# Moving the loads of the gates' weights and of y into the first batch, and the first filter stores to SyncE

## The chip, the cores and the metric

One core of a Trainium2 chip. The time is the device time of one call in microseconds (us), median of several runs. The kernel before took 1970.6 us (1967.1 to 1972.8), so one run alone says little about less than 3 us.

Names in the profile: PE is TensorE's matmul, PEld its weight load, DVE VectorE, ACT ScalarE, POOL GpSimd, SP SyncE. A q behind an engine's name is its sequencer, which issues transfers. A half-rate window is a stretch for which the trace gives PE's granted clock as 0.5; before the kernel's end such windows last 3.4 us each, and some come two in a row (6.8 us). Work at half rate takes twice its time, so 3.4 us of it cost 1.7 us. L404 is a line of the kernel; since all matmuls are recorded by one helper, matmuls are told apart by their tiles (`acc<-V,wb`).

## The reference, cut to what matters

A layer norm and a ReLU over x of shape (64, 256, 256), then one graph layer per graph: a 1-wide and a 17-wide convolution with batch norms, a message pass over `A = exp(-dist) * adj`, and a GRU.

```python
h = jnp.maximum(_layernorm(x, axis=-1), 0.0)
...
    h = _bn(_conv1d(h, conv2_w, 8), bn2_g, bn2_b, bn2_m, bn2_v)      # 17 taps
    x_conv = jnp.transpose(jax.nn.relu(h + xc), (0, 2, 1))
    ...
    gi = x_in @ w_ih.T + b_ih
    gh = x @ w_hh.T + b_hh
    ...
    return (1.0 - z) * nn_ + z * x
# x = x + that
```

## The kernel before

The 17-wide convolution is done by a short transform along the sequence (VectorE), products per frequency (TensorE) and the transform back. The 57 steps of `filters` compute the transformed filters on TensorE, ScalarE copies each result to one of six `fo` buffers, and a store puts it into device memory. `load_bin` later reads the filter of one frequency back as a tile `wb` (768 KB), of which there are three buffers. The filters are computed once; the batches (8 batches of 4 pairs of graphs) follow.

```python
    def filters(m, g):
        ...
        t = stage.tile([P, W], FP, name="fo", bufs=6)
        nc.scalar.copy(t[:size * kinds], p[:size * kinds])
        (nc.gpsimd if g % 2 else nc.sync).dma_start(
            out=filt[m][g * KG:g * KG + size].rearrange("k t c o -> (k t) (c o)"), in_=t[:size * kinds])
...
    for j in range(PB):                      # the first batch's convolutions; 4 filter steps in each
        ...
        for m, n in steps[j * 4:(j + 1) * 4]:
            filters(m, n)
    forward()                                # queues VectorE's odd and even transforms
    for j, (m, n) in enumerate(steps[PB * 4:]):      # the other 41 filter steps
        filters(m, n)
        if j + PB * 4 == 2 * NG - 10:
            load_bin(0, 0)
            load_bin(0, 1)
    nc.scalar.dma_start(out=w_hh, in_=hh_wT.rearrange("(k p) o -> p k o", p=P))
    nc.scalar.dma_start(out=w_ih, in_=ih_wT.rearrange("(k p) o -> p k o", p=P))
    ...
    load_y(0)                                # x once more, for the residual: GpSimd's queue
    load_y(1)
    pace.flush(odd)                          # VectorE: the odd transform
    s2, h2_shift = fold_bn(bn2, "bn2", 1.0 / L)      # VectorE, one pow on GpSimd, VectorE
    ...
    for b in range(NB):
        i = b * PB
        embed(i)
        products(b, 0)                       # the even transform is put between these on VectorE
        message(i)
        products(b, 1)
        affinity(i)                          # ends with GpSimd's load of the next adj
        embed(i + 1)
        products(b, 2)
        transpose_a(i)
        products(b, 3)
        aggregate(i)
        products(b, 4)
        message(i + 1)
        products(b, 5)
        affinity(i + 1)
        ...                                  # products 6 and 7, then gates(): first use of w_hh, w_ih
```

Of the kernel before, what the change touches and what calls it, by code (L numbers as in the profile page):

```python
# [297 lines left out]
def kernel(  # L298
# [26 lines left out]
    nc = tc.nc  # L325
    P = 128
# [43 lines left out]
    def load_rows(t, src, i, eng):  # L370
        for g in range(G):
            eng.dma_start(out=row_tile(t, g), in_=rows(src, G * i + g))  # L372
# [9 lines left out]
    def load_y(i):  # L382
        Y[i] = late.tile([P, G * MC, D], FP, name="y", bufs=2)
        load_rows(Y[i], x, i, nc.gpsimd)
# [18 lines left out]
    def mm(p, w, v, columns, **kw):  # L403
        nc.tensor.matmul(p, w, v, **kw)  # L404
        pace.tensor(columns)
# [87 lines left out]
    for n, bins in enumerate(PASSES):  # L493
        f = filter_points(bins, TAPS)
        m = np.zeros((KG, TAPS, KG, f.shape[1]), np.float32)
# [26 lines left out]
    def aux():  # L522
        return psum.tile([P, W], FP, name="aux", bufs=3)

    def acc():
        return psum.tile([P, W], FP, name="acc", bufs=5)
# [41 lines left out]

    filt = [dram.tile([P, t.shape[1] // KG, DC, D], FP, name=f"filt{n}") for n, t in enumerate(points)]

    def filters(m, g):

        kinds = filt[m].shape[1]
        size = min(KG, P - g * KG)
        p = acc()
        for dc in range(DC):
            mm(p[:size * kinds, dc * D:(dc + 1) * D], points[m][:size * TAPS, :size * kinds],
               taps[:size * TAPS, g, dc, :], D, start=True, stop=True)
        t = stage.tile([P, W], FP, name="fo", bufs=6)
        nc.scalar.copy(t[:size * kinds], p[:size * kinds])  # L580
        (nc.gpsimd if g % 2 else nc.sync).dma_start(  # L581
            out=filt[m][g * KG:g * KG + size].rearrange("k t c o -> (k t) (c o)"), in_=t[:size * kinds])


# [2 lines left out]
    def load_bin(b, n):  # L587
        b, n = b + n // BINS, n % BINS
        if b < NB:
            WB[b, n] = work.tile([P, 3, DC, D], FP, name="wb", bufs=3)  # L590
            kinds, m = 3 if n < BINS - 1 else 2, n // len(PASSES[0])
            first = 3 * (n - PASSES[m][0])
            nc.sync.dma_start(out=WB[b, n][:, :kinds], in_=filt[m][:, first:first + kinds])
# [15 lines left out]
    def products(b, m):  # L609
        load_bin(b, 2 * m + 2)  # L610
        p = [acc() for _ in range(3)]
        for n in range(2):
            for kind, v in enumerate(operands(2 * m + n)):
                if v is None:
                    continue
                for o in range(DC):
                    for k in range(DC):
                        mm(p[kind][:, (n * DC + o) * P:(n * DC + o + 1) * P],
                           WB[b, 2 * m + n][:, kind, k, o * P:(o + 1) * P],
                           v[:, k::DC, 0, :], P, start=(k == 0), stop=(k == DC - 1))  # L620
        load_bin(b, 2 * m + 3)
        p1 = work.tile([P, W], FP, name="p1")
        pv = [t.rearrange("p (n a e) -> p a n e", n=2, e=NW) for t in (p1, p[1], p[2])]
        if m < 7:
            nc.scalar.copy(p1, p[0])
            if m < 4:
                re, im = Yv(m % 2, m // 2 * 2, 2), Yv(m % 2, 4 + m // 2 * 2, 2)
            elif m < 6:
                re, im = Yu(m - 4, 0, 2), Yu(m - 4, 2, 2)
            else:  # L630
                t = Yu.t[:, :, :, 6:8, :].rearrange("p a c n e -> p n a c e")
                re, im = t[:, 0], t[:, 1]
            pace.vector(2 * W, pace.pe + PSUM)
            nc.vector.tensor_sub(re, pv[0], pv[2])
            nc.vector.tensor_add(im, pv[0], pv[1])
        else:
            half = W // 2
            nc.scalar.copy(p1[:, :half], p[0][:, :half])
            nc.scalar.mul(Yu(0, 4)[:, :, 0, :], p[0][:, half:].rearrange("p (a e) -> p a e", e=NW), 0.5)
            nc.scalar.mul(Yu(1, 4)[:, :, 0, :], p[1][:, half:].rearrange("p (a e) -> p a e", e=NW), 0.5)  # L640
            pace.vector(W, pace.pe + PSUM)
            nc.vector.tensor_sub(Yu(0, 5)[:, :, 0], pv[0][:, :, 0], pv[2][:, :, 0])
            nc.vector.tensor_add(Yu(1, 5)[:, :, 0], pv[0][:, :, 0], pv[1][:, :, 0])
# [59 lines left out]
    def aggregate(i):  # L703
        XNM[i] = late.tile([P, DC, W], FP, name="xnm", bufs=2)
        for dc in range(DC):
            p = aux()
            for g in range(G):
                for c in range(MC):
                    mm(graph(p, g), MSG[i][:, g, c, dc * P:(dc + 1) * P], AT[i][:, g, c, :], N,
                       start=(c == 0), stop=(c == MC - 1))  # L710
            nc.scalar.activation(XNM[i][:, dc, :], p, AF.Copy)
# [76 lines left out]
    w_ih = const.tile([P, 2 * DC, 3 * D], FP)  # L788
    w_hh = const.tile([P, DC, 3 * D], FP)
# [17 lines left out]
    for j in range(PB):  # L807
        if j > 0:
            transpose_h(j)
        if 0 < j < PB - 1:  # L810
            norm(j + 1)
        conv1(j)
        run(split_steps(j))
        for m, n in steps[j * 4:(j + 1) * 4]:
            filters(m, n)
    forward()
    for j, (m, n) in enumerate(steps[PB * 4:]):
        filters(m, n)
        if j + PB * 4 == 2 * NG - 10:
            load_bin(0, 0)  # L820
            load_bin(0, 1)
    nc.scalar.dma_start(out=w_hh, in_=hh_wT.rearrange("(k p) o -> p k o", p=P))
    nc.scalar.dma_start(out=w_ih, in_=ih_wT.rearrange("(k p) o -> p k o", p=P))
    stage_ctx.close()
    late = ctx.enter_context(tc.tile_pool(name="late", bufs=1, reuse_waits="tile"))
    Yvt = late.tile([P, SL], FP, name="Yv")
    Yv = Slots(Yvt, GB * DC, L // 2, NW)
    load_y(0)
    load_y(1)
    pace.flush(odd)  # L830
    s2, h2_shift = fold_bn(bn2, "bn2", 1.0 / L)
    b_rz = const.tile([P, 2 * DC], FP)
# [5 lines left out]
    for b in range(NB):  # L838
        i = b * PB
        nxt = i + PB  # L840
        embed(i)
        pace.flush(odd)
        products(b, 0)
        message(i)
        products(b, 1)
        pace.add(fft.branch_back(Yv, T, 0))
        affinity(i)
# [3 lines that stand above are left out]
        if b > 0:  # L851
            finish(i - 1)
        products(b, 3)
        pace.flush(even)
        pace.add(fft.branch_back(Yv, T, 2))
        pace.add(fft.odd_back(Yv, T))
        aggregate(i)
        products(b, 4)
        message(i + 1)
        products(b, 5)  # L860
        pace.add(mix(fft.q_back(Yu, T), fft.odd_factors(Yv)))
        affinity(i + 1)
        norm(nxt)
        products(b, 6)
        transpose_a(i + 1)
        products(b, 7)
        pace.add(mix(fft.p_back(Yu, T), fft.q_factors(Yu)))

        def join(j):
            pace.add(fft.join(Yu, Yv, T, slice(2 * G * j, 2 * G * (j + 1))))  # L870
            pace.add([(W, lambda o=o: residual(i + j, o)) for o in range(DC)], joined[j])
        stats, scale = norm_steps(nxt + 1)
        join(0)
        pace.add(stats)
        join(1)
        pace.add(scale, normed)
        pace.add(split_steps(nxt), halved)
        join(2)
        join(3)
        aggregate(i + 1)  # L880
        transpose_h(nxt)
        embed(i + 2)
        message(i + 2)
        conv1(nxt)
        affinity(i + 2)

        def wait(j=0):
            pace.flush(joined[j])
        gates(i, 0, wait)
        transpose_a(i + 2)  # L890
        gates(i, 1)
        pace.flush(normed)
        transpose_h(nxt + 1)
        aggregate(i + 2)
        pace.flush(halved)
        conv1(nxt + 1)
        stats, scale = norm_steps(nxt + 2)
        pace.add(stats)
        pace.add(split_steps(nxt + 1), halved)
        pace.add(scale, normed)  # L900
        pace.flush(joined[1])
        gates(i + 1, 0)
        pace.flush(normed)
        transpose_h(nxt + 2)
        message(i + 3)
        embed(i + 3)
        conv1(nxt + 2)
        stats, scale = norm_steps(nxt + 3)
        pace.add(stats)
        pace.add(split_steps(nxt + 2), halved)  # L910
        pace.add(scale, normed)
        finish(i)
        gates(i + 1, 1)
        affinity(i + 3)
        gates(i + 2, 0)
        pace.flush(normed)
        transpose_h(nxt + 3)
        transpose_a(i + 3)
        conv1(nxt + 3)
        pace.add(split_steps(nxt + 3), halved)  # L920
        if b + 1 < NB:
            forward()
        finish(i + 1)
        gates(i + 2, 1)
        aggregate(i + 3)
        gates(i + 3, 0)
        finish(i + 2)
        gates(i + 3, 1)
# [46 lines left out]
```

## Time and profile before

| | before |
|---|---|
| time, median | 1970.6 us |
| span of the profiled run | 1969.0 us |
| PE busy | 1918.9 us (97 %) |
| PE's waits after the first filter store, to 220 us | 10.6 us in nine places, 0.6 of them for hT in two |
| PE's waits after 220 us | 2.2 us |

PE is the bound nearly everywhere, so the span splits at two landmarks. The last filter matmul starts at 112.16 us. From there to the first gates' matmul (`acc<-hT,w_hh`, at 197.83 us) it is 85.7 us. From there to the end it is 1771.2 us. The change touches only the first two stretches. The profile's lines stand in the prediction, with their reading. Two names in it: msg is the operation of VectorE that empties one of three `aux` buffers, for which PE waits; the fold (`fold_bn`) is the string of tiny operations that makes scale and shift of the second batch norm, with bn_scale on GpSimd in its middle.

### The profile page before, as it was taken

The page shows a single profiled execution, that of the slowest core. Times are in us where ns is not written, and L with a number is a line of the kernel's source. Part 1 is how long each engine was busy: PE and PEld are TensorE (multiplying, and loading weights), DVE is VectorE, ACT ScalarE, POOL GpSimd, SP SyncE. Part 2 cuts the span into 40 slices and gives each one's busy share as a digit, 9 for nine tenths or more (in the row PEclk, how much of TensorE's full clock was granted, in tenths as well). Part 3 has the DMA queues.
Part 4 walks back from the last instruction along what each step waited for, and adds up shares of the span by engine and source line. Part 5 has one row for each costly group of instructions (what it writes and reads, how often), then busy time and mean ns, then how long its engine had stood idle before and what let it go on. Part 6 is the DMA issues. An engine that isn't in the chain of part 4 may idle for free.

```text
span 1969.0 us, 21300 instructions
## 1 busy us (share of the span) xinstructions
PE 1918.9 (97%) x7972; PEld 1209.2 (61%) x7972; DVE 1402.3 (71%) x2668; ACT 641.9 (33%) x1050; POOL 184.9 (9%) x277
## 2 busy tenths in 40 slices
PE   4899999999999999999999999999999999999997
PEld 2678555875459655695557855496546955478543
DVE  2769738996489946998379964899559984699522
ACT  1443322343222432235222433124322253234321
POOL 3210000010100000010000101001010100000000
PEclk9999999999999999999999999999999999999999
DMA  5776011540216212270115402163122711144010
GB/s 177 224 233 185 22 43 59 182 129 22 70 35 224 74 43 59 86 223 24 43 48 165 156 12 70 42 207 93 32 70 59 241 36 34 32 132 143 4 43 22
DMA packets 67967, 187.12 MB, mean 95 GB/s; under 512 B 20606, under 2 KB 25470, under 8 KB 67865
## 3 DMA queue, kind: packets, MB, share of 16 engines
q1 hardware_dynamic: 32812, 123.61, 19.1%
q0 software_dynamic: 29808, 56.13, 10.5%
q10 hardware_dynamic: 5245, 6.02, 1.0%
q8 instruction: 62, 1.02, 0.2%
q14 instruction: 40, 0.33, 0.1%
HBM read 156.55 MB, written 29.10 MB: 94 GB/s over the span
## 4 chain that ended last, share of the span: by engine, by line
PE 92%; DMA 4%; issue 2%; DVE 1%; POOL 0%; ACT 0%; POOLq 0%; ACTq 0%; DVEq 0%
PE acc L404 72%; PE aux L404 17%; PE aux L408 4%; DMA taps<-in_c_wT_dram 1%; DMA w_ih<-in_ih_wT_dram 1%; DMA filt<-fo 1%; DMA x<-in_x_dram 0%; DMA wb<-filt 0%; POOL filt L581 0%; DMA w_c<-in_c_wT_dram 0%; ACT fo L580 0%; POOL rstd L433 0%; POOL out_dram L767 0%; DVE x L436 0%; DVE st L427 0%
## 5 line engine op out<-in xcount | busy, mean ns | idle before, releaser
L404 PE MATMUL acc<-hT,w_hh 128*128 128x512 f32 x768 | 350.6, 592 | 0.0
L404 PE MATMUL acc<-xnm,w_ih 128*128 128x512 f32 x768 | 350.4, 592 | 0.0
L404 PE MATMUL acc<-Yv,w_ih 128*128 128x512 f32 x768 | 340.0, 592 | 0.0
L404 PEld LDWEIGHTS acc<-xnm,w_ih 128*128 128x128 f32 x768 | 145.9, 190 | 183.7 <-issue 183.7
L404 PEld LDWEIGHTS acc<-Yv,w_ih 128*128 128x128 f32 x768 | 145.9, 190 | 183.7 <-issue 181.5
L404 PEld LDWEIGHTS acc<-hT,w_hh 128*128 128x128 f32 x768 | 143.4, 190 | 157.8 <-issue 151.4
L739 ACT ACTIVATE tr<-acc,b_rz 128x512 f32<-128x512 f32 x64 | 44.0, 687 | 556.8 <-PE acc L404 556.8
L741 DVE SCALAR_TENSOR_TENSOR gn<-tr,gn 128x512 f32<-128x512 f32 x64 | 44.2, 691 | 235.4 <-ACT tr L739 235.4
L404 PE MATMUL acc<-hT,w_c 128*128 128x512 f32 x256 | 120.5, 615 | 13.6 <-ACT hT L537 13.6
L404 PE MATMUL acc<-V,wb 128*128 128x128 f32 x1024 | 125.9, 276 | 0.0
L404 PE MATMUL acc<-U,wb 128*128 128x128 f32 x1024 | 122.1, 275 | 0.0
L404 PEld LDWEIGHTS acc<-U,wb 128*128 128x128 f32 x1024 | 120.0, 192 | 1.2
L404 PEld LDWEIGHTS acc<-V,wb 128*128 128x128 f32 x1024 | 120.7, 194 | 0.0
L58 DVE SCALAR_TENSOR_TENSOR V<-T,V 128x256 f32<-128x256 f32 (+2 forms) x224 | 119.8, 610 | 0.3
L404 PE MATMUL aux<-w_msg,hT 128*128 128x256 f32 x512 | 115.8, 379 | 0.0
L404 PE MATMUL aux<-aT,msg 128*128 128x256 f32 x512 | 115.8, 379 | 0.0
L404 PEld LDWEIGHTS aux<-w_msg,hT 128*128 128x128 f32 x512 | 95.5, 190 | 16.3 <-issue 4.7
L404 PEld LDWEIGHTS aux<-aT,msg 128*128 128x128 f32 x512 | 95.5, 190 | 15.9 <-issue 4.1
L767 POOL DMA_DIRECT2D out_dram<-y x64 | 39.2, 616 | 696.6 <-DVE y L766 696.6
L372 POOL DMA_DIRECT2D adj<-in_adj_dram x62 | 37.3, 606 | 620.2 <-DVE e L690 606.6
L404 PEld LDWEIGHTS acc<-hT,w_c 128*128 128x128 f32 x256 | 49.7, 198 | 68.1 <-issue 49.3
L766 DVE TENSOR_TENSOR y<-aux,y 128x512 f32<-128x512 f32 x64 | 41.2, 685 | 61.5 <-PE aux L408 61.5
(131 smaller groups left out, 2720.7 us busy)
## 6 DMA issues: line engine op xcount, KB each, us to landing
wb<-filt SPq DMA_DIRECT2D x120, 768.0 KB
y<-in_x_dram POOLq DMA_DIRECT2D x64, 256.0 KB, 4.1
out_dram<-y POOLq DMA_DIRECT2D x64, 256.0 KB, 5.1
adj<-in_adj_dram POOLq DMA_DIRECT2D x62, 256.0 KB, 4.3
x<-in_x_dram SPq DMA_DIRECT2D x60, 256.0 KB
filt<-fo POOLq DMA_DIRECT2D x18, 252.0 KB, 4.5
filt<-fo SPq DMA_DIRECT2D x18, 252.0 KB
wb<-filt SPq DMA_DIRECT2D x8, 512.0 KB
```

What stands on the lines that cost most here:

```text
L58: return self.step(out, lambda: self.v.scalar_tensor_tensor(out, x, s, y, op0=ALU.mult, op1=ALU.add))
L372: eng.dma_start(out=row_tile(t, g), in_=rows(src, G * i + g))
L404: nc.tensor.matmul(p, w, v, **kw)
L408: nc.tensor.transpose(p, v, ident)
L739: nc.scalar.activation(tr, pr, AF.Tanh, bias=b_rz[:, dc:dc + 1], scale=0.5)
L741: nc.vector.scalar_tensor_tensor(gn, tr, 1.0, gn, op0=ALU.add, op1=ALU.mult)
L766: nc.vector.tensor_add(row_tile(Y[i], g), p, row_tile(Y[i], g))
L767: nc.gpsimd.dma_start(out=rows(out, G * i + g), in_=row_tile(Y[i], g))
```

## The change

The intent: take the gates' weights (2.3 MB) and the y tiles (1 MB) out of the moment when the first batch starts and its wb tiles are urgent, and free GpSimd's queue of the first filter stores.

```diff
-    def filters(m, g):
+    def filters(m, g, eng):
 ...
-        (nc.gpsimd if g % 2 else nc.sync).dma_start(
+        eng.dma_start(
 ...
         for m, n in steps[j * 4:(j + 1) * 4]:
-            filters(m, n)
+            filters(m, n, nc.sync)
     forward()
     for j, (m, n) in enumerate(steps[PB * 4:]):
-        filters(m, n)
+        filters(m, n, nc.gpsimd if j % 2 else nc.sync)
 ...
-    nc.scalar.dma_start(out=w_hh, in_=hh_wT.rearrange("(k p) o -> p k o", p=P))
-    nc.scalar.dma_start(out=w_ih, in_=ih_wT.rearrange("(k p) o -> p k o", p=P))
 ...
-    load_y(0)
-    load_y(1)
     pace.flush(odd)
 ...
         aggregate(i)
+        if b == 0:
+            nc.gpsimd.dma_start(out=w_hh, in_=hh_wT.rearrange("(k p) o -> p k o", p=P))
+            nc.gpsimd.dma_start(out=w_ih, in_=ih_wT.rearrange("(k p) o -> p k o", p=P))
+            load_y(0)
+            load_y(1)
         products(b, 4)
```

## The prediction

> **What bounds the kernel now.** I read the page first. Its first part makes TensorE the bound of the whole:
>
> ```profile
> PE 1918.9 (97%) x7972; PEld 1209.2 (61%) x7972; DVE 1402.3 (71%) x2668; ACT 641.9 (33%) x1050; POOL 184.9 (9%) x277
> ```
>
> Only 50 us of 1969 are not PE, so the question is where PE idles and whether the change touches that place. The view of waits, PE alone, for 0 to 220 us and then for 220 to 2000 us, says that nearly all of it lies at the start:
>
> ```profile
> PE acc L404 <- ACT hT L537: 13.6, 3, 13.0
> PE aux L408 <- DVE x L436: 12.5, 2, 10.9
> PE acc L404 <- ACT h L550: 4.1, 1, 4.1
> PE acc L404 <- DMA wb<-filt: 3.6, 3, 2.9
> PE acc L404 <- ACT fo L580: 3.1, 2, 2.9
> PE aux L404 <- DVE msg L675: 1.7, 1, 1.7
> ```
>
> After 220 us there is one wait of 2.2 us. The first two groups and the third (4.1 us, until 38.8 us) lie before the first filter store at 40.7 us: the change cannot reach them. The rest is 3.6 + 3.1 + 1.7 us and the 1.6 us left of the second group, 10.0 us in all. Next, the timeline of PE, for where these lie:
>
> ```profile
> 94.73 1.09 PE L404 MATMUL acc<-taps,points 119*77 119x256 f32 x4 [2.88 <-ACT fo L580]
> ...
> 126.06 1.73 PE L404 MATMUL acc<-Sv,wb 128*128 128x128 f32 x8 [2.85 <-DMA wb<-filt]
> 127.58 3.02 PE L404 MATMUL acc<-V,wb 128*128 128x128 f32 x16
> 130.87 1.16 PE L404 MATMUL acc<-Sv,wb 128*128 128x128 f32 x8 [0.27 <-DMA wb<-filt]
> 131.86 1.95 PE L404 MATMUL acc<-V,wb 128*128 128x128 f32 x16
> ...
> 136.36 1.83 PE L404 MATMUL aux<-rd,ld 67*128 67x256 f32 x4 [1.68 <-DVE msg L675]
> ...
> 150.30 1.16 PE L404 MATMUL acc<-Sv,wb 128*128 128x128 f32 x8 [0.49 <-DMA wb<-filt]
> ```
>
> The gates' weights (w_hh 768 KB, w_ih 1536 KB) go out on ScalarE's queue at 112.6 and 113.1 us, and the wait at 126.06 for a spectral weight tile wb, issued at 113.55, is the sign of their crowding. But removing a wait helps only if no later wait takes its place, and one does: at 136.36 PE waits for VectorE's msg. So I looked at VectorE in its timeline. It runs without a gap from 116.5 us to 152.6 us, and what it waited for before that is
>
> ```profile
> 116.54 0.16 DVE L471 TENSOR_TENSOR bn_scale<-bn_scale,bn_g 128x2 f32<-128x2 f32 x1 [20.71 <-POOL bn_scale L470]
> ```
>
> a tiny operation of GpSimd, whose own timeline shows why it is late:
>
> ```profile
> 112.52 0.53 POOL L581 DMA_DIRECT2D filt<-fo  x1 [1.07 <-DMA filt<-fo]
> 113.35 2.42 POOL L372 DMA_DIRECT2D y<-in_x_dram  x4 [0.30 <-issue]
> 115.74 0.76 POOL L470 TENSOR_TENSOR bn_scale<-bn_scale,neg_half 128x2 f32<-128x2 f32 x1
> ```
>
> It stands in GpSimd's program behind the last filter store and four y loads. From its end to the msg that frees PE at 136.36 there are 19.8 us of VectorE work without a hole. This, not the transfers, is the path that sets the end between 112 and 136 us. (The chain of waits names the w_ih transfer there instead, 19.9 us ending at 132.93; VectorE is busy up to that moment and beyond, so I don't believe the attribution: the wait was over when VectorE arrived.)
>
> **What the Trainium skill says.** "DMA: Bandwidth & Descriptors", section "Issuing engines are not separate DMA queues": all queues end on the same 16 engines, so moving a load to another queue doesn't make it cheaper; only its moment counts. The trace agrees: in 120 to 130 us the view by windows has the DMA share at 1.03 and 288 GB/s. "TensorE: Matmul & The Clock Gate", Part 1: after idling, PE runs at half rate for a free-running window of about 3.4 us. The trace agrees: the granted clock is 0.83 in 120 to 130 and 130 to 140 us (3.4 us at half in 10 gives 0.83), and 16 V,wb matmuls take 3.02 us at 127.58 against 1.95 at 131.86, with the 8 before them 1.73 against 1.05. A gap therefore costs about 1.07 + 0.68 = 1.75 us more if PE is the bound after it. "SBUF — State Buffer" warns that VectorE in a two-port mode can starve GpSimd's descriptor writing; GpSimd's issues take 0.53 us beside a busy VectorE here, so I charge nothing.
>
> **The change part by part.** (The order of instructions in the built programs confirms each move.)
>
> (a) The y loads leave the place before bn_scale. Removed from the path: 4 x 0.60 = 2.42 us, and the 0.30 us before them that belonged to the first y load's waits. After the last store ends at 113.05, bn_scale takes 0.76 and VectorE starts near 113.85 instead of 116.54: 2.7 us. All of VectorE's string, and so the msg, moves by that. **Gain 2.7 us.**
>
> (b) w_hh, w_ih and y (2304 + 1024 KB) leave 112 to 138 us. The waits of 2.85 and 0.27 us for wb vanish, but PE then reaches the msg about 3.1 us sooner, plus 1.75 us for the half-rate window, and waits there: one gap in place of two. **Gain 0 on the path**, and a half-rate window after 136 remains (rd,ld takes 1.83 us for four there against 1.03).
>
> (c) They arrive instead on GpSimd behind the adjacency load of the second pair of graphs, some 1.5 us after it starts, near 144 us: issue about 0.8 us for w_hh (256 rows; w_se with as many rows took 0.79) and 1.2 for w_ih (my estimate). First use of w_hh is at 197.8 us, of w_ih at 201.3: over 50 us, while 2.3 MB at 95 GB/s (the third left beside wb of a 290 GB/s total) need 24 us. In time. But wb is read on SyncE's queue in just these 40 us: 11 tiles, about 8.4 MB; with adj, weights and y 12.2 MB in 43 us is 280 GB/s, close to the 283 to 335 GB/s that the packets reach in 5 us stretches while the weights load. A tile has 6 to 10 us from the matmul that frees its buffer to its use, and needs 4 at two thirds of the rate; but at 113 us it took 12.5 us behind the same weights. So a stall of 0 to 5 us after 145 us, where VectorE is no longer the bound from 153 us on, is possible. I charge **1 us of loss**, and count the present 0.49 us at 150.30 as **gained**, because the backlog of w_ih that delayed that tile is gone.
>
> (d) The first 16 stores: eight leave GpSimd for SyncE. The issue costs 0.31 us on SyncE against 0.53, on nobody's path. But PE's gap before 52.2 us hangs on the third x tile:
>
> ```profile
> 49.34 0.75 DVE L427 BATCH_NORM_STATS2 st<-x 128x6 f32<-128x256 f32 x2 [1.96 <-DMA x<-in_x_dram]
> ...
> 52.20 1.74 PE L408 MATMUL aux<-ident,x 128*128 128x128 f32 x8 [1.59 <-DVE x L436]
> ```
>
> That tile comes on ScalarE's queue and in 40 to 50 us shares the engines with two GpSimd stores (504 KB) and SyncE's traffic. With the two behind SyncE's adjacency loads, the tile should land about 1 us sooner: 1 us, and perhaps one chance in three to lose the half-rate window at 55 us (1.7 us). **Gain 1.5 us.**
>
> (e) The later stores alternate by their running number: in the second pass even groups go to GpSimd, odd ones to SyncE, the reverse of before. The gap of 2.88 us at 91.85 ends with a copy that waited 3.98 us for a buffer whose store GpSimd issued at 84.53, just beside the first two wb loads, and which landed only at 94. With the parity turned, that store sits on SyncE ahead of wb and the next one is the slow one: one step of four matmuls (4 x 0.215) is won. **Gain 0.9 us.**
>
> Sum: 2.7 + 0.5 + 1.5 + 0.9 - 1.0 = 4.6 us. 1970.6 - 4.6 = 1966.0.
>
> **The rivals.** R1, the crowding only moves: weights on GpSimd's queue delay wb tiles at 150 to 170 us, where PE is the bound, by up to 5 us plus a half-rate window of 1.75. For it: the 12.5 us of the tile at 113. Against it: then the filter stores' backlog lay in front of the tile too. It would give about 1971. R2, the wb wait was the bound: then 2.85 + 0.27 + 1.75 come off, with (a) and (d), (e) about 10 us, 1961. Against it: the unbroken VectorE string. R3, stores all on SyncE are slower: SyncE's first store waits until 43.51 us for an unrelated tap load (10.1 us in SyncE's waits), and four stores queue behind the adjacency loads; a copy held for a buffer would hold ScalarE's next copy of hT. There 2.2 us of slack stand (ScalarE waited 2.26 us for PE at 53.53), so it should cost nothing; if it does, (d) becomes -1 and the time 1968.5.
>
> **Range and chances.** Without (d) and (e) and with R1 it is 1971.5 at most; with R2 or both half-rate windows gone 1959.5. Runs of before spread over 5.6 us. Two per cent is 39 us: all of PE's waits within the change's reach are 10 us, so faster by 2% is out, and 39 us of new stalls would need every wb tile late. Same 0.98, the rest 0.01 each.
>
> **What would show it.** bn_scale right behind the last store, VectorE's wait there 2 to 3 us shorter relative to the last store; no wb wait before the msg, a longer msg wait (about 3 us); PE's acc<-V,wb and U,wb after 145 us without waits over 1 us; the first hT,w_hh matmul not waiting; the gaps at 52 and 92 us smaller. Wrong would be: wb waits of several us between 145 and 180 us, or a filter phase that ends later relative to its start.

## The result, and the profile after

The changed kernel took 1968.42 us (1967.42 to 1970.62, 6 runs) against 1970.62 us of the kernel before. The ratio is 0.9991, with a 95 % interval from 0.9978 to 1.0004. A ratio is the mean time of one kernel's fast runs over that of the other's of the same rounds, so it is not quite the ratio of the medians. Measured again later (below), it was 0.9994. The time lies in the predicted range, and the change is not told apart from none by the times alone. The profiles tell more.

The page's first part of the changed kernel:

```profile
PE 1915.0 (97%) x7972; PEld 1206.6 (61%) x7972; DVE 1402.1 (71%) x2668; ACT 641.0 (33%) x1050; POOL 182.3 (9%) x272
```

The same 7972 matmuls took 3.9 us less. They do the same work, so this should be time at half rate that fell away; the two traces' clock records have 25.7 us at half rate against 32.3, worth 3.3 us. Now PE's view of waits from 0 to 220 us (us in total, times, longest):

```profile
PE aux L408 <- DVE x L436: 11.0, 1, 11.0
...
PE aux L404 <- DVE msg L675: 4.3, 1, 4.3
PE acc L404 <- ACT fo L580: 3.9, 4, 1.3
PE acc L404 <- DMA wb<-filt: 3.4, 3, 2.0
PE acc L404 <- DVE Yv L61: 0.4, 1, 0.4
```

The msg wait grew from 1.7 to 4.3 us, the wait for fo buffers from 3.1 to 3.9, the one for wb is about as long as before, and the second wait for the x tile is gone (before, this line says 12.5 us, 2 times). GpSimd's timeline shows the moved loads, which now stand behind bn_scale:

```profile
109.09 0.73 POOL L470 TENSOR_TENSOR bn_scale<-bn_scale,neg_half 128x2 f32<-128x2 f32 x1
138.55 1.27 POOL L372 DMA_DIRECT2D adj<-in_adj_dram  x2 [28.73 <-DVE e L690]
139.81 0.75 POOL L855 DMA_DIRECT2D w_hh<-in_hh_wT_dram  x1
140.55 0.80 POOL L856 DMA_DIRECT2D w_ih<-in_ih_wT_dram  x1
141.35 2.42 POOL L372 DMA_DIRECT2D y<-in_x_dram  x4
```

VectorE's timeline shows the end of its wait for bn_scale:

```profile
109.86 0.16 DVE L471 TENSOR_TENSOR bn_scale<-bn_scale,bn_g 128x2 f32<-128x2 f32 x1 [17.68 <-POOL bn_scale L470]
```

That is at 109.86 instead of 116.54 us, 6.7 us sooner: 4.0 us because the filters end sooner in this profile, 2.6 us because y is gone. PE's timeline shows where these 6.7 us went:

```profile
129.69 2.07 PE L404 MATMUL aux<-rd,ld 67*128 67x256 f32 x4 [4.29 <-DVE msg L675]
...
144.67 1.16 PE L404 MATMUL acc<-Sv,wb 128*128 128x128 f32 x8 [0.34 <-DMA wb<-filt]
...
151.48 2.92 PE L404 MATMUL acc<-U,wb 128*128 128x128 f32 x24 [0.41 <-DVE Yv L61]
155.47 2.94 PE L404 MATMUL acc<-U,wb 128*128 128x128 f32 x24 [1.08 <-DMA wb<-filt]
...
166.52 2.94 PE L404 MATMUL acc<-U,wb 128*128 128x128 f32 x24 [1.97 <-DMA wb<-filt]
...
196.42 3.60 PE L404 MATMUL acc<-hT,w_hh 128*128 128x512 f32 x8
```

At the msg PE is 6.67 us ahead of before (129.69 against 136.36). At the first gates' matmul, 196.42 us, only 1.4 us are left. About 5.3 us were handed back in between: 3.8 us in these four later waits against 0.5 us before, and the rest largely at half rate. Each of the waits for wb costs some 0.2 us more than its figure, because the ends of matmuls normally lie beside the next ones: 24 matmuls in an unbroken row take 2.68 us from start to start (48 take 5.36), from 151.48 to 155.47 it is 3.99, so 1.31 us were lost where the line says 1.08. The view by windows of the changed kernel, for PE alone, shows the half rate and the traffic (columns: stretch, its length, PE busy, granted clock, DMA share, GB/s):

```profile
126.00:130.00 4.00, 0.32 (x1) 0.84 0.43 171
130.00:134.00 4.00, 4.00 (x7) 0.50 0.00 0
134.00:138.00 4.00, 4.00 (x27) 0.81 0.00 0
138.00:142.00 4.00, 4.00 (x38) 1.00 0.72 215
```

PE works at half rate from 129.69 to 135.55 us, which costs half of 5.9 us; before, one window of 3.4 us cost 1.7. The DMA engines stand idle from 130 to 138 us, and then all the moved loads come at once. Their packets, added up from the two traces by the time of their end (SyncE's queue carries wb):

```
before  115:120 us  SyncE  75  GpSimd  43  ScalarE 203 GB/s
        120:125            145          56           84
        125:130            152          46           86
after   145:150 us  SyncE 157  GpSimd 220  ScalarE   0 GB/s
        150:155            194         217            0
        155:160            122         135            0
```

The packets' starts, counted per us, show more than these sums. Before, from 120 to 130 us, SyncE's queue moved 247 packets of 6144 bytes of wb, and ScalarE's 273 packets of 3072 bytes of the weights. After, from 146 to 155 us, it was 289 packets of 6144 bytes on SyncE's queue and 302 on GpSimd's, where the same weights come in packets of 6144 bytes too. The numbers of packets are nearly even both times, so wb had two thirds of the bytes of the two before and half after.

There is more: from 142 to 145 us, while adj's packets (4096 bytes) came on GpSimd's queue, SyncE's moved 3, although a wb tile had been issued at 140.80 us; and from 157 to 159 us, as y's packets (4096 bytes) began to come in numbers, it moved 12. Behind adj it nearly stood before the change too (21 packets from 147 to 149 us). Why it nearly stood is not shown.

At the x tile, VectorE's statistics of its second half come at 47.40 us instead of 49.34 (VectorE's timeline), and PE starts its transposes without a gap at 50.25 us:

```profile
47.40 0.75 DVE L427 BATCH_NORM_STATS2 st<-x 128x6 f32<-128x256 f32 x2 [0.75 <-DMA x<-in_x_dram]
```

### The profile page after: what moved, and what is told of

It is laid out like the page before. It is cut to its first block, busy times and chain, and to the rows that moved or that the text cites. A ratio compares the mean times of both kernels' runs of the same rounds, so it can differ in the third digit from the quotient of the medians.

```text
span 1968.3 us, 21290 instructions
## 1 busy us (share of the span) xinstructions
PE 1915.0 (97%) x7972; PEld 1206.6 (61%) x7972; DVE 1402.1 (71%) x2668; ACT 641.0 (33%) x1050; POOL 182.3 (9%) x272
## 3 DMA queue, kind: packets, MB, share of 16 engines
q0 software_dynamic: 29632, 56.50, 10.4%
## 4 chain that ended last, share of the span: by engine, by line
PE 90%; DMA 4%; issue 3%; DVE 2%; POOL 1%; ACT 0%; POOLq 0%; DVEq 0%; ACTq 0%
PE acc L404 70%; PE aux L404 16%; PE aux L408 4%; DMA taps<-in_c_wT_dram 1%; DMA wb<-filt 1%; DMA x<-in_x_dram 1%; POOL filt L581 0%; DMA filt<-fo 0%; DVE U L58 0%; DMA w_c<-in_c_wT_dram 0%; DVE PT L61 0%; DVE U L64 0%; DVE T L64 0%; DVE T L61 0%; DVE st L427 0%
```

## The experiments

Twelve runs were made, two of them of the kernels before and after once more. With the first profiles of before and after they give 14 profiles; the table is read from them. "Filters end" is the start of the last filter matmul, "to gates" the time from there to the first `acc<-hT,w_hh`. What follows took 1769.8 to 1771.9 us in every profile. So the span is the sum of three numbers, of which the last is nearly constant. "x gap" is PE's wait ahead of the third x tile, "fo waits" the sum of PE's waits for fo buffers, counting gaps over 0.25 us.

| kernel | time, median | ratio (95 %) | x gap | fo waits | filters end | to gates |
|---|---|---|---|---|---|---|
| before | 1970.6 | | 1.59 | 2.88 | 112.2 | 85.7 |
| before again | 1972.6 | 1.0007 (0.9995 to 1.0019) | 1.35 | 2.72 | 111.3 | 88.1 |
| changed | 1968.4 | 0.9991 (0.9978 to 1.0004) | none | 3.90 | 108.1 | 88.3 |
| changed again | 1971.0 | 0.9994 (0.9979 to 1.0008) | none | 3.35 | 110.8 | 88.5 |
| stores only | 1970.4 | 0.9995 (0.9983 to 1.0008) | 0.73 | 2.45 | 112.6 | 87.2 |
| loads only | 1970.5 | 0.9996 (0.9983 to 1.0010) | 1.57 | 2.43 | 110.1 | 89.6 |
| changed, loads later | 1966.8 | 0.9978 (0.9965 to 0.9992) | 0.85 | 3.92 | 112.5 | 84.2 |
| changed, fold early | 1961.3 | 0.9954 (0.9941 to 0.9968) | 0.66 | 3.33 | 108.2 | 78.1 |
| changed, both mends | 1958.4 | 0.9934 (0.9923 to 0.9946) | none | 3.43 | 107.9 | 76.9 |
| before, fold early | 1965.6 | 0.9974 (0.9962 to 0.9987) | 0.79 | 2.43 | 109.6 | 81.9 |
| before, y behind fold | 1966.2 | 0.9978 (0.9966 to 0.9990) | 2.87 | 3.34 | 113.7 | 83.2 |
| before, 2 stores moved | 1968.1 | 0.9985 (0.9970 to 1.0001) | none | 2.98 | 108.7 | 85.8 |
| before, later stores' parity | 1971.4 | 0.9999 (0.9983 to 1.0015) | 0.84 | 4.20 | 111.6 | 86.0 |
| changed, y later | 1967.6 | 0.9979 (0.9966 to 0.9991) | none | 2.55 | 110.1 | 84.8 |

All outputs were correct. Three groups ran on one chip each, with their own runs of the kernel before: stores only, loads only, loads later and fold early; before again, changed again, y behind fold and both mends; and the last four that remain. The ratios refer to these runs of before (medians 1971.8, 1971.8 and 1971.3 us), that of the row "changed" to the six runs of before beside it. What an experiment says of a wait rests on one profile.

The filters' end wanders from 107.9 to 113.7 us, and the traces' clock records say with what. Between 46 us and the filters' end there is no half-rate window in the three profiles that end at 107.9 to 108.2 us (changed, fold early, both mends), 3.4 us in the four that end at 108.7 to 111.6, 6.8 us in the five at 110.1 to 112.5, and 10.2 us in the two at 112.6 and 113.7 (stores only, y behind fold). The three without one have their fo waits in four gaps of at most 1.3 us; the other eleven have one of 1.8 us or more, and each is followed by 3.4 or 6.8 us at half rate. So compare the filters' end only with this beside it.

### The stores alone (e1_stores_only)

```diff
 # the changed kernel, with
+    nc.scalar.dma_start(out=w_hh, ...)      # where they were before
+    nc.scalar.dma_start(out=w_ih, ...)
+    load_y(0); load_y(1)                    # where they were before
-        if b == 0: (the block of four loads)
```

> The filter stores as in the changed kernel, the gates' weights and y loaded as before. Theory (the change has two independent gains before 137 us and one later loss, and the loss belongs to the moved loads): the filter phase ends about 4 us sooner than before (near 108.5 us instead of 112.5), GpSimd's bn_scale starts near 111.7 instead of 115.7 (the y loads are in front of it again), and from there everything as before, so the time is about 4 us below before, 1966.5 us, and 2 us below the changed kernel. Rival (the earlier end of the filter phase was chance, the place of PE's half-rate windows in that one execution): bn_scale within 2 us of before and a time of 1969 to 1971 us.

Measured: 1970.41 us, ratio 0.9995. The filter phase ended at 112.63 us, no sooner than before. The first theory falls in its first half: the same arrangement of stores that ended at 108.1 us in the changed kernel ended 4.5 us later here. In this profile PE had half-rate windows at 54 us (3.4 us) and 95 us (6.8 us); the changed kernel's first profile had none there. So much of the 4 us at the filters' end was not the change's. The time and bn_scale's start (116.21 us against 115.74) are the rival's. The gap at the x tile did shrink, to 0.73 us.

### The loads alone (e2_loads_only)

```diff
 # the changed kernel, with every store as before
-            filters(m, n, nc.sync)
+            filters(m, n, nc.gpsimd if n % 2 else nc.sync)
-        filters(m, n, nc.gpsimd if j % 2 else nc.sync)
+        filters(m, n, nc.gpsimd if n % 2 else nc.sync)
```

> The loads as in the changed kernel, all filter stores as before. Theory: bn_scale starts 2.6 us sooner than before at an unchanged end of the filter phase, PE waits 3 to 4 us for msg, and then gives back about 3.5 us in waits for wb between 143 and 170 us; net the time is within 1.5 us of before, 1969 to 1972 us. Rival (the moved loads cost nothing after 140 us, my prediction's term): 3 us below before, 1967.5 us.

Measured: 1970.53 us, as the theory has it. PE waits 4.2 us for msg and 4.1 us for wb. The stretch to the gates is 89.6 us, longer than in either profile of before (85.7, 88.1). The moved loads gain nothing on the whole.

### The loads later (e3_loads_late)

```diff
 # the changed kernel: the block of four loads moved on
         aggregate(i)
-        if b == 0: (the block of four loads)
         products(b, 4)
         ...
         affinity(i + 1)
+        if b == 0: (the block of four loads)
```

> The changed kernel with the block of four loads moved behind the affinity of the second pair of graphs, so that GpSimd issues them near 175 us, when the first batch's last wb tiles are mostly loaded. Theory (the weights crowd wb): PE's waits for wb between 143 and 170 us (3.4 us in the changed kernel) fall under 0.7 us, hT,w_hh starts about 3 us sooner than in the changed kernel and still without waiting for its weights, time about 3 us below the changed kernel, 1965.5 us. Rival (the wb waits come from the filter phase's pace or from wb's own rate, not from the weights): the waits stay over 2 us and the time stays at 1968.4 us. Second rival: the weights come too late and PE waits for them at 193 us.

Measured: 1966.81 us, ratio 0.9978, a clear gain on before. The weights were issued at 175.7 and 176.4 us and nobody waited for them. The stretch to the gates is 84.2 us against 88.3 and 88.5. PE's waits for wb and for msg, from the view of waits to 220 us of this kernel:

```profile
PE aux L404 <- DVE msg L675: 4.2, 1, 4.2
...
PE acc L404 <- DMA wb<-filt: 0.9, 1, 0.9
```

The wb waits fell from 3.4 to 0.9 us, a little more than the 0.7 us I had allowed; the one left is at 149 us, before the moved loads are issued. The moved loads were what delayed wb. The median is 1.3 us above the 1965.5 expected; this profile's filters ended at 112.5 us.

### The fold early (e4_fold_early)

```diff
+    s2, h2_shift = fold_bn(bn2, "bn2", 1.0 / L)
     forward()
     ...
-    s2, h2_shift = fold_bn(bn2, "bn2", 1.0 / L)
```

> The changed kernel with the second batch norm's fold (the little DVE and GpSimd operations around bn_scale) moved ahead of the odd transform, so that VectorE need not wait for GpSimd's last filter store. Theory (VectorE's string after bn_scale bounds 109 to 130 us): PE's wait for msg of 4.3 us vanishes together with most of the half-rate window after it (3.4 us lost over 6.8 us at half), so PE stands about 7 us earlier at 130 us; but the weights still crowd wb afterwards and may take back 3 to 5 us more than now, because PE comes sooner: time 1962 to 1966 us. Rival (wb or the filter stores bound this stretch and msg is only the last to be seen): the msg wait turns into wb waits of the same length and the time stays within 1 us of 1968.4.

Measured: 1961.34 us, just under the theory's 1962 to 1966. All of PE's waits from 0 to 220 us in this kernel:

```profile
PE acc L404 <- ACT hT L537: 14.0, 3, 13.4
PE aux L408 <- DVE x L436: 11.4, 2, 10.8
PE acc L404 <- ACT h L550: 5.1, 1, 5.1
PE acc L404 <- ACT fo L580: 3.3, 4, 1.1
PE acc L404 <- DMA wb<-filt: 1.2, 2, 0.7
```

The msg wait is gone, and no wb wait took its place between 108 and 143 us. After the filters PE has no half-rate window until the kernel's end. VectorE's string behind bn_scale was the bound of that stretch. The wb waits didn't grow as I feared. It may be that the loads come at a better moment (argued, not shown): VectorE is also done with the adjacency sooner, so GpSimd issues the loads at 130.8 us, 9 us sooner than in the changed kernel.

### Before and after once more (r_before, r_after)

> The kernel before once more, for a second profile. The runs so far suggest that the end of the filter phase wanders from execution to execution (108.1 to 112.6 us, the same arrangement of stores giving 108.1, 108.2, 112.5 and 112.6), with the place of PE's half-rate windows. Theory: the wait ahead of the third x tile's transposes is 1.6 us again (1.59 and 1.57 with half of the first stores on GpSimd), the filter phase ends anywhere between 108 and 113 us, and from there to the first hT,w_hh matmul it takes 85 to 87.5 us again. Rival (the filter phase's end belongs to the arrangement of stores): it ends within 0.5 us of 112.2.

> The changed kernel once more, for a second profile and a paired time. Theory: the x tile's wait under 0.9 us again, the filter phase's end anywhere between 108 and 113 us, from there to the first hT,w_hh matmul 88 to 90 us (88.3 and 89.6 in the two profiles with the moved loads), wb waits of 3 to 4.5 us between 143 and 170 us, time 1 to 2.5 us below before. Rival (the moved loads gain on the whole): 83 us from the filter phase's end to hT,w_hh.

Measured: before again 1972.56 us and filters' end at 111.25 us; changed again 1970.99 us and 110.75 us. The second profile of the changed kernel lost 2.6 us of the filters' end that the first had, which settles that a part of it is chance (here a fo wait of 2.8 us was followed by 6.8 us at half rate). By medians the changed kernel was 0.8 us below before, a little less than the 1 to 2.5 I expected. The second profile of before took 88.1 us to the gates, 0.6 us more than expected: there PE had two half-rate windows after the msg wait (6.8 us) where the first had one. The changed kernel's stretch was 88.5 us, as expected of the theory and not of the rival.

### The y loads behind the fold (e7_y_behind_fold)

```diff
 # the kernel before, with
-    load_y(0)
-    load_y(1)
     pace.flush(odd)
     s2, h2_shift = fold_bn(bn2, "bn2", 1.0 / L)
+    load_y(0)
+    load_y(1)
```

> The kernel before with nothing but the four y loads moved behind the second batch norm's fold in program order; the weights stay on ScalarE's queue at 112 us and the stores as before. Theory (my term (a) alone): bn_scale starts 1.0 us after the last filter matmul's start instead of 3.6; the msg wait of 1.7 us vanishes and PE is then held by the same wb waits as before at 126 and 131 us, so from the filter phase's end to hT,w_hh 82.5 to 84.5 us instead of 85.7, time 1.5 to 3.5 us below before, better than the changed kernel from that point on. Rival (the string of VectorE is not what holds PE): 85.7 us and the time of before.

Measured: 1966.21 us, ratio 0.9978; 83.2 us to the gates, as the theory says. bn_scale starts 0.9 us after the last filter matmul's start. The ratio means 4.3 us less than before, somewhat more than the 1.5 to 3.5 I expected. PE's waits from 40 to 220 us are:

```profile
PE acc L404 <- DMA wb<-filt: 3.7, 2, 3.3
PE acc L404 <- ACT fo L580: 3.3, 1, 3.3
PE aux L408 <- DVE x L436: 2.9, 1, 2.9
PE acc L404 <- ACT hT L537: 0.3, 1, 0.3
```

Without the msg wait, the 3.3 us for wb at 128 us is now what holds PE: the weights on ScalarE's queue do delay wb, but before the change this was mostly hidden behind VectorE. By its ratio, this two-line move is worth more than the whole change.

### Both mends together (e5_fold_loads)

```diff
 # the changed kernel with e4's and e3's edits
```

> The changed kernel with both mends: the fold ahead of the odd transform and the block of loads behind the second pair's affinity. Theory: no msg wait, no half-rate window after the filters, wb waits under 0.5 us (1.16 us with the fold alone): 1960 us, about 1 us below the fold alone. Rival: the loads now come too late (they are issued near 165 us, and the first use of w_hh is near 186 us), and PE waits for the weights: above 1962 us.

Measured: 1958.43 us (1957.4 to 1960.3), ratio 0.9934: faster than both kernels, by medians of the same group 13.4 us below before and 12.6 us below the changed kernel. PE waited 0.6 us for wb (I had allowed 0.5) and for no weights, which were issued at 163.8 and 164.6 us; the first gates' matmul started at 184.8 us.

### The fold early in the kernel before (e6_fold_before)

```diff
 # the kernel before with e4's edit
```

> The kernel before, with only the fold of the second batch norm moved ahead of the odd transform; stores and loads as before. Theory: VectorE's string no longer holds PE, so what is left is what the old place of the loads costs: waits for wb of 4 to 6 us in all between 118 and 150 us and one or two half-rate windows (1.7 us each); from the filter phase's end to hT,w_hh 81 to 84 us (78.1 with the fold and the loads where the change put them), time 1964 to 1967 us. Rival (the loads at 112 us are harmless, and only the string mattered): 78 us and 1961 us.

Measured: 1965.57 us and 81.9 us to the gates, as the theory says. Waits for wb were 3.2 us, less than the 4 to 6 expected, with one half-rate window behind the first (2.6 us, at 123 us). With VectorE out of the way, the old place of the loads costs 3.8 us more than the new one (81.9 against 78.1 us; the two kernels differ in the order of the stores as well). So the idea of the change is right once the bound in front of it is gone; in this kernel it came too early.

### Two stores (e8_first4)

```diff
 # the kernel before, with
-            filters(m, n)
+            filters(m, n, nc.gpsimd if n % 2 and j > 0 else nc.sync)   # j counts groups of four
```

> The kernel before with only the two GpSimd stores of the first four moved to SyncE; everything after as before. Theory: these two are what the third x tile shared the engines with, so the tile's second half is worked on near 48 us (47.4 to 48.7 in the six profiles with all 16 on SyncE, 48.7 to 49.8 in the four without) and PE's wait ahead of its transposes is under 0.9 us instead of 1.35 to 2.9. Rival (the later stores or GpSimd's queue matter): the wait stays over 1.3 us. The time cannot tell this apart: within 2 us of before.

Measured: VectorE's timeline of this kernel shows

```profile
47.48 0.75 DVE L427 BATCH_NORM_STATS2 st<-x 128x6 f32<-128x256 f32 x2 [0.62 <-DMA x<-in_x_dram]
```

and PE had no gap ahead of the transposes. The two stores that went from GpSimd to SyncE are enough. The time, 1968.10 us, is about 3 us below before by its ratio, more than the 2 us I had allowed, with 1 just inside the interval. Over all profiles, the statistics of the tile's second half start at 49.33 us on average in the six kernels with those two stores on GpSimd (48.70 to 49.78) and at 47.91 us in the eight with them on SyncE (47.40 to 48.65). PE's gap is 1.50 us (0.79 to 2.87) against 0.28 us (none to 0.85).

### The later stores' parity (e10_parity)

```diff
 # the kernel before, with
-        filters(m, n)                                            # n % 2 decides
+        filters(m, n, nc.gpsimd if j % 2 else nc.sync)           # the later 41 steps
```

> The kernel before with only the later stores alternating by running number. My prediction's term (e) says PE's waits for buffers in the filter phase fall from 2.4 to 3.3 us by 0.9 us. Theory now (the stores are held back by the transfers' total rate, not by the place of one store): their sum stays between 2.4 and 4 us, as in the profiles of the changed arrangement (2.5 to 3.9).

Measured: 1971.35 us, ratio 0.9999, waits for fo buffers of 4.2 us: a miss for my term (e), and just above the 2.4 to 4 us of the new theory too. Over all profiles the waits are 2.80 us on average in the six with the old order and 3.39 us in the eight with the new one. The new order wins nothing here.

### Only y later (e11_y_late)

```diff
 # the changed kernel: only y moved on
             nc.gpsimd.dma_start(out=w_ih, ...)
-            load_y(0)
-            load_y(1)
 ...
         affinity(i + 1)
+        if b == 0:
+            load_y(0)
+            load_y(1)
```

> The changed kernel with only the four y loads moved on, behind the second pair's affinity; the weights stay at 140 us. It tells which of the moved loads delays wb. If the weights do (2304 of 3328 KB): waits for wb of 2.5 to 4 us between 143 and 170 us remain, the time is within 1 us of the changed kernel. If it is simply the sum of bytes: the waits fall by about a third, by 1 to 1.5 us. If y does: the waits fall under 1 us.

Measured: 1967.60 us, ratio 0.9979; waits for wb of 1.5 us instead of 3.4, 84.8 us to the gates. This falls between what I had written for "the sum of bytes" (1.9 to 2.4 us) and for "y does" (under 1 us). y is a third of the bytes and took away more than half of the waits. Two profiles of a wait that moves by about 1 us don't settle the shares. The packets speak for y, though: in the three profiles with y right behind the weights, SyncE's queue has two us with 9 to 13 packets in all once y comes (157 to 159 us in the changed kernel, 160 to 162 and 159 to 161 in changed again and loads only); here every us from 145 to 162 has 17 or more. And y, first used at 261.5 us in the changed kernel, had no reason to stand there.

## Why the prediction was right or wrong

The predicted time was 1966.0 us in a range of 1959.5 to 1971.5; measured 1968.4, and 1971.0 in a later group. "Within 2 %" held, and the range did too. The working behind it held only in part: the sum of -4.6 us is made of terms of which two failed, and the loads' half of the change comes out with the wrong sign. That the time lies so near is in part luck: the terms as measured add up to almost +2 us (below), not to -2.

**What bounds it: right.** VectorE's string behind bn_scale sets the end of 112 to 136 us. It takes 20.60 us from bn_scale's start to the freed matmul in the changed kernel and 20.62 before. The fold early removes it and PE's wait with it, in both kernels. The distrust of the chain of waits, which gave this stretch to w_ih, was justified.

**(a) bn_scale ahead of y, gain 2.7 us: right.** From the last filter matmul's start to bn_scale's start it is 0.97 us instead of 3.58, so 2.6 us. Done alone (y behind the fold) it shortens the stretch to the gates to 83.2 us from 85.7 and 88.1.

**(b) the wb waits at 126 and 131 us give nothing on the path: right, with one term too small.** They vanished and msg took their place. I foresaw "a half-rate window after 136 remains", one of 3.4 us. The longer gap, 4.2 to 4.3 us, was followed by two in all five profiles that have it: 6.8 us, of which PE worked 5.9 at half rate in the changed kernel's first profile and 4.6 to 5.6 in the others. In the first that costs 2.9 us instead of 1.7, so 1.2 us. It isn't all the change's: of the old arrangement's shorter gaps, those of 2.6, 3.0 and 3.9 us were followed by two windows as well, those of 1.7 and 2.9 us by one.

**(c) the loads' new place, +0.5 and -1.0 us: wrong, and this is what ate the gain.** The step that failed is that a tile "needs 4 at two thirds of the rate". Taken from the traces' semaphores (a tile has landed with the sixteenth update after its issue), the five wb tiles issued from 140.8 to 158.5 us landed 10.4 to 13.2 us after their issue; before, the six issued from 143.6 to 162.1 us took 4.2 to 8.1. Two things are in that.

First, two thirds was wb's share beside ScalarE's queue, with its packets half as large (64 % of the packets' bytes of the two queues from 120 to 130 us, before). On GpSimd's queue the weights' packets are as large as wb's: from 145 to 155 us wb got 157 and 194 GB/s, GpSimd's loads 220 and 217, less than half for wb. So the working's "only its moment counts" was too simple. The total was higher than the 290 of the term, though, so these rates are not far from its 193 GB/s. Second, the term had nothing for the stretches in which SyncE's queue nearly stood: it moved 3 packets from 142 to 145 us, where at the 32 a us of the stretch from 146 us some 90 of a tile's 128 would have come (an estimate). How much of the wait is due to which is not shown.

The tiles came late for the products of 151 to 169 us: PE started at 155.47 and 166.52 us on tiles that landed at 155.4 and 166.5. The present 0.49 us did not vanish. The later waits came to 3.8 us against 0.5: a loss of 3.3 us, and 0.6 us more for the broken rows of three more waits, where I had 0.5 in all. Rival R1 was the right description for that stretch. Moving the loads on takes most of it away again. Taken together, the loads' half is -2.6 + 1.2 + 3.3 + 0.6 = +2.5 us, and the profiles agree: 88.3 against 85.7 us to the gates in the first two, and 88.8 us on average with the loads in the new place (88.3, 88.5, 89.6) against 86.6 us in the five with the old place, fold and y order (85.7, 88.1, 87.2, 85.8, 86.0), which is +2.2.

**(d) the first stores, 1.5 us: right in mechanism.** The tile comes 1.4 us sooner, PE's gap shrinks by 1.2 us, and two stores alone do it. The half-rate window near 54 us is there in two of the eight profiles with this arrangement and in three of the six without, too few to say that it is the change's doing. It was absent in both profiles of the changed kernel.

**(e) the parity of the later stores, 0.9 us: wrong.** The step that failed is "that store sits on SyncE ahead of wb and the next one is the slow one: one step is won". The sum of the waits for buffers did not fall (3.4 us on average against 2.8). I take it that the stores, 252 KB each 0.86 us or 293 GB/s, then outrun the total rate, which no order of queues changes; that is argued, and was not shown by a run of its own.

Two slips of the working: PE's waits within reach were 10.6 us and not 10.0, since the first group (hT) has two waits of 0.6 us together at 54 and 64 us, after the first store. And the range's upper end doesn't follow from its terms: without (d) and (e) and with R1's 5 and 1.75 us it is 1970.6 - 2.7 + 6.75 = 1974.7, and R1 with (d) and (e) gives 1972.3 and not 1971. By the terms as measured the time would have been about 1972.3, just outside, so that the range held is luck as well.

What stays open: the time of the change itself. Two groups gave 0.9991 and 0.9994, both with 1 inside the interval. The terms as measured, -1.2 for the x tile, +0.6 for the fo buffers and +2.2 to +2.5 for the loads, would make it almost 2 us slower, while the times are 1 to 2 us lower. The runs' granted clocks say where that lies: they average 0.9935 over the 12 runs of the changed kernel and 0.9928 over 34 of before, by which PE was 25.6 us at half rate against 28.4, worth 1.4 us; the core's span differs by 1.6 us (1967.8 against 1969.4). So nearly all of the small difference is time at half rate. Fewer windows in the filter phase fit that: the changed kernel's first profile has none there, and its second two. But three of the seven profiles with all of the new order of stores have none, four have 6.8 us or more, and whether the new order is what splits the fo waits into short ones is not shown.

## What to carry to other kernels

Before moving transfers away from a wait, look at which wait ends last after it; here a tiny GpSimd operation behind a queue of transfer issues held VectorE for 20 us and PE with it, and doing that operation earlier was worth more than the change; with the loads mended too it was 13 us. A load that is moved needs a place where the engines are idle and its neighbours aren't urgent: ask who shares the rate there, compare the sizes of the packets on the two queues (here half for the other queue, not a third), and look at the packets per us for stretches in which one queue nearly stands. For effects of 2 us in 2000, compare landmarks in several profiles, because one profile shows one pattern of half-rate windows, and count these windows before a stretch is called shorter.

## What the Trainium skill lacked or had wrong

- "TensorE: Matmul & The Clock Gate", Part 1, has the clock fall after an idle window of about 3.4 us, and warns of idle gaps above that; for shorter gaps it gives no size. Here much shorter gaps were followed by half rate: 1.7 us (the msg wait before) by one window of 3.4 us, and each of eleven fo waits of 1.8 to 3.5 us by 3.4 or 6.8 us. Gaps of 4.2 to 4.3 us were followed by 6.8 us in five of five profiles; four gaps of 0.7 to 1.3 us in the filter phase of the changed kernel by none. There is no clean limit: of the gaps of 0.7 to 1.6 us at the third x tile, four were followed by a window near 54 us and four were not.
- "DMA: Bandwidth & Descriptors", section "SWDGE vs HWDGE vs iDMA", gives a preferred packet of at most 4096 B for GpSimd's queue. The trace has 6144 B packets on it for w_hh and w_ih, as large as SyncE's for wb; from ScalarE's queue the same loads came in packets of 3072 B. That the packet depends on the issuing queue, and with it the share, the page doesn't say. The same page's "Queues, rings and completion order" has the engines go round the queues packet by packet. The trace agrees for the weights beside wb (nearly even numbers of packets, 273 and 247 before, 302 and 289 after), but beside the 4096 B packets of adj and y SyncE's queue moved only 3 packets from 142 to 145 us and 12 from 157 to 159 us; whether it had one ready in these us the trace doesn't say.
- "SBUF — State Buffer" warns that VectorE, in its two-port modes, keeps GpSimd from writing the descriptors of its transfers. No run here shows it: the issues of w_hh and w_ih took 0.75 and 0.80 us beside a working VectorE; in which mode it worked the trace doesn't say.
